# The load of the spread offsets three steps later in a band's chain, with its reader left in place

## The chip, the cores and the metric

The kernel runs on one core of a Trainium2 chip. The metric is the device time of one execution in microseconds. The core's engines are TensorE (PE, with its weight loads shown as PEld), VectorE (DVE), ScalarE (ACT), GpSimd (POOL) and SyncE (SP), which here only issues DMAs.

## The reference

Two layers run one after the other on a batch of 32 images of 96 channels and 56 x 56 pixels, in float32.

- Layer 0: a 1x1 convolution to 576 channels, batch norm, SiLU; a depthwise 3x3 convolution, batch norm, SiLU; a squeeze-and-excite gate; a 1x1 convolution back to 96 channels, batch norm, and the input is added.
- Layer 1: a channel gate from the magnitude of a Fourier transform and a spatial gate from means and that spectrum; the gated image `y`; a 3x3 convolution that gives 18 offsets per pixel and a gate; a plain 3x3 convolution `y_base`; a deformable convolution; a mix of the two; batch norm over the whole batch; the input added; ReLU.

The deformable part is what the change touches:

```python
off = offset.reshape(b, 9, 2, h, w)
px = xx + off[:, :, 0]
py = yy + off[:, :, 1]
sampled = _grid_sample_taps(y, px, py)          # bilinear
y_def = jnp.einsum('bcthw,oct->bohw', sampled, def_w.reshape(c, c, 9))
z = (1 - gate) * y_base + gate * y_def
```

## The kernel before

**Three streams at once.** In `layers`, image `b` is in layer 1's convolutions, image `b+1` in the end of layer 0 and in the gates (`attend`), and image `b+2` in the start of layer 0 (`hidden`). The convolutions are worked off in bands of 8 rows: 7 bands per image, 224 in all. Each band has two halves, each half 7 tiles of 4 columns. For each half TensorE samples the tiles with small matmuls (`sample_tiles`, L738, with transposed blocks from `block_channels`, L724) and then applies the deformable weights (`deform`, L757) into one PSUM tile `pd`, of which there is a single buffer. `combine` (first instruction L796) reads `pd` on VectorE and makes the band's `z`.

**Steps.** After each tile the loop advances two things by one step: `more`, which is the generator `offsets` of the band two ahead (`find(n + 2)`), and `pump()`, which advances the two other streams in proportion to the slots that have passed and runs actions that were put off (`later`). A band advances `more` once at its beginning and 14 times in its halves, so every `yield` in `offsets` is one place between two tiles.

**The chain of one band's offsets.** `offsets` makes the joint convolution on TensorE (L615), copies the 18 offsets to `at` (L664, VectorE), writes them to `od` in DRAM (L668, queue of POOL), makes the rest of `y_base` (L644), takes the largest offset (L675), lets some steps pass, and loads `od` into `ht` (L680, queue of SP). The load spreads each row of `od` to 8 groups of partitions, 252 KB into 112 partitions. After more empty steps it puts off `hats`, which runs two slots later: ScalarE makes `ho` from `ht` (L686, L688) and stores it to `hd` in DRAM (L690, queue of ACT). `ho`'s first instruction is kept in program order on ScalarE.

**The weights.** `prepare` loads, per half band, two `wc` (L702) and one `wr` (L703) from `hd` through the queue of SP; `weights` multiplies them on VectorE (L709, kept in program order), and L738 reads the product. For one half `prepare` needs the `hd` of the next band.

**What else SP issues.** The queue of SP has a fixed order, that of the program text as it is run (`manual_schedule`). Between the loads named above stand those of the other streams: `hq<-h2d` for the 1x1 convolution back (`project_loads`, L311, 784 KB for the first half of the rows and 980 KB for the second, each into a single buffer), `hq<-x1d` for the Fourier transform (L369, 98 KB each, two to a group), `yp<-x1d` and `yp<-fqd` (L594, L606) and `xt` (L213). L329 and L335 are the matmuls that read the first kind, L396 those that read the second. The order on the other engines is made by a scheduler from the program text and priorities.

**Buffers.** `ht` and `ho` have one buffer each; `wc` has three and `wr` two.

Of the kernel before, what the change touches and what calls it, by code (L numbers as in the profile page):

```python
# [628 lines left out]
def joint_conv(nc, p, yp, j, hid):  # L629


    w = p["w"]
    pa = bank(p)
    conv3(nc, pa[:, :BW], w["joint"], yp, CJ, j)
    nc.scalar.activation(hid, pa[:DMID, :BW], AF.Relu, bias=w["dg1b"][:DMID])  # L635
    yb = p["yb"].tile([C, BW], FP, name="yb")
    nc.scalar.activation(yb[BC:], pa[OFF0 + QC :, :BW], AF.Identity, bias=w["cv"]("base_b")[BC:])
    yield yb, pa[OFF0 : OFF0 + NOFF, :BW]
    pb = bank(p)
    for k in range(NTAP):  # L640
        dy, dx = divmod(k, 3)
        r0 = j * RB + dy + PD - 1
        for i in range(2):
            nc.tensor.matmul(pb[i * BC : (i + 1) * BC, : BW // 2].rearrange("p (h w) -> p h w", h=RB // 2), w["base"][:, k],  # L644
                             yp[:C, r0 + i * RB // 2 : r0 + (i + 1) * RB // 2, dx + PD - 1 : dx + PD - 1 + W],
                             start=(k == 0), stop=(k == NTAP - 1))
    yield
    for i in range(2):
        nc.scalar.activation(yb[:BC, i * BW // 2 : (i + 1) * BW // 2], pb[i * BC : (i + 1) * BC, : BW // 2], AF.Identity,  # L649
                             bias=w["cv"]("base_b")[:BC])  # L650
    yield


def offsets(nc, p, yp, j, top, hid, ybs, hds, defer):

    w = p["w"]
    joint = joint_conv(nc, p, yp, j, hid)
    yb, pa = next(joint)  # L660
    ybs.append(yb)
    at = p["off"].tile([NOFF, NTX, 2, TP], FP, name="at")
    for s in range(2):
        nc.vector.tensor_copy(at[:, :, s].rearrange("o t (r c) -> o t r c", r=TS),  # L664
                              pa[:, s * BW // 2 : (s + 1) * BW // 2].rearrange("o (r t c) -> o t r c", r=TS, t=NTX))
    yield
    od = p["dp"].tile([NTX, 2, NOFF, TP], FP, name="od")
    nc.gpsimd.dma_start(od.rearrange("t s o p -> o (t s) p"), at.rearrange("o t s p -> o (t s) p"))  # L668
    yield
    next(joint)  # L670
    yield
    next(joint)
    yield
    next(joint, None)
    nc.vector.tensor_reduce(top, at.rearrange("o t s p -> o (t s p)"), AX.X, ALU.max, apply_absolute_value=True)  # L675
    for _ in range(4):
        yield
    ht = p["ht"].tile([SB * NTX, 4, KP], FP, name="ht")
    src = od.rearrange("t s o p -> t (s o p)").unsqueeze(0).to_broadcast([SB, NTX, 4 * KP])
    nc.sync.dma_start(ht.rearrange("q n k -> q (n k)"), src)  # L680
    for _ in range(6):
        yield

    def hats():
        ho = p["ht"].tile([SB * NTX, 2, 2, KP], FP, name="ho")
        p["tc"].keep_in_program_order(nc.scalar.activation(  # L686
            ho.rearrange("q x s n -> q s x n"), ht.rearrange("q (s x) n -> q s x n", s=2), AF.Abs, bias=w["blk"]))
        nc.scalar.activation(ho, ho, AF.Relu, bias=w["one"], scale=-1.0)  # L688
        hd = p["dp"].tile([2, 2, SB, NTX, KP], FP, name="hd")
        nc.scalar.dma_start(hd.rearrange("x s i t n -> (i t) (x s) n"), ho.rearrange("q x s n -> q (x s) n"))  # L690
        hds.append(hd)

    defer(hats)
# [259 lines left out]
def layers(tc, a, dp, x1d, zd, stats, far):  # L953
# [8 lines left out]
    with ExitStack() as ctx:  # L962
# [127 lines left out]
        def find(n):  # L1090
            if n % 2 == 0:
                hids.append(p["hid"].tile([2 * NS, BW], FP, name="hid"))
            hid = hids[n // 2][n % 2 * NS : n % 2 * NS + DMID]
            return offsets(nc, p, yp, bands[n][1], top[:, n % NBD : n % NBD + 1], hid, ybs, hds,
                           lambda hats: later.append((slot + 2, hats)))
# [420 lines left out]
```

## Time and profile before

| | |
|---|---|
| median of 3 runs | 9001.68 us (8979.61 to 9002.55) |
| profiled execution, own time | 8993.57 us |
| its span | 8991.8 us |
| mean granted TensorE clock | 0.94 |
| PE busy | 8180.0 us (91% of the span) |
| DVE busy | 7174.8 us (80%) |
| ACT busy | 5380.8 us (60%) |
| POOL busy | 2600.4 us (29%) |
| queue of SP (q1) | 985.20 MB, 46.7% of 16 DMA engines' span |
| queue of ACT (q10) | 329.80 MB, 10.2% |
| queue of POOL (q0) | 162.60 MB, 6.7% |

Busy times are of one execution and overlap between engines. In the lists of waits each line names the engine and line that stood idle, what ended the idle time, and then the total in us, the number of times and the longest. In the timeline the columns are start, duration, engine, line, operation, output and inputs, with the idle time before it and what ended it in brackets. In the table by windows each engine's busy time and count of instructions is followed by the granted clock, the share of the DMA engines and GB/s.

### The profile page before, as it was taken

The numbers are of one execution on the slowest core, as the hardware profiler recorded it, in microseconds if no ns is written. First come the engines' busy times: TensorE is split into PE (matmuls) and PEld (weight loads), VectorE is DVE, ScalarE is ACT, GpSimd is POOL, SyncE is SP. The second block draws the span as 40 slices with busy tenths as digits, with TensorE's granted clock in tenths as the row PEclk, the third lists the DMA queues.
The fourth block names the chain that finished last, engine by engine and source line by source line (L and its number), as shares of the span: only waits on it lengthen the run. The fifth ranks groups of instructions, "written<-read, shape, count | busy, mean of one in ns | idle before, by whom it ended". The sixth has DMA issues, their size and how long they took to land. (4 is left out here: it accounts for less than half of the span.)

```text
span 8991.8 us, 137403 instructions
## 1 busy us (share of the span) xinstructions
PE 8180.0 (91%) x52406; PEld 5185.1 (58%) x52406; DVE 7174.8 (80%) x6821; ACT 5380.8 (60%) x10486; POOL 2600.4 (29%) x2608
## 2 busy tenths in 40 slices
PE   5899999999999999999999999999999999999960
PEld 3456565666656656665666666566566656666640
DVE  7688888888888888888888888888888888887333
ACT  2356666666666666666666666666666666666553
POOL 0133233333323332332332333233333323332210
PEclk9889999999999999999999999999999999999985
DMA  2356666666666666666666666666666666666669
GB/s 80 109 144 167 164 167 164 164 155 155 169 167 167 169 163 150 159 164 167 169 167 160 153 159 166 168 167 168 164 151 162 166 166 168 168 165 146 130 189 417
DMA packets 1068756, 1486.47 MB, mean 165 GB/s; under 512 B 590190, under 2 KB 839838, under 8 KB 1055806
## 3 DMA queue, kind: packets, MB, share of 16 engines
q1 hardware_dynamic: 858995, 985.20, 46.7%
q10 hardware_dynamic: 153803, 329.80, 10.2%
q0 software_dynamic: 55296, 162.60, 6.7%
q8 instruction: 420, 6.88, 0.4%
q14 instruction: 242, 1.98, 0.1%
HBM read 1064.29 MB, written 412.65 MB: 164 GB/s over the span
## 5 line engine op out<-in xcount | busy, mean ns | idle before, releaser
L262 DVE SCALAR_TENSOR_TENSOR acch<-hp,w,acch 128x1512 f32<-128x1512 f32 (+1 forms) x2250 | 4348.3, 1933 | 38.3
L615 PE MATMUL mm<-yp,c_jointW 104*128 104x448 f32 x4032 | 1655.9, 562 | 1.0 <-DMA yp<-fqd 1.0
L720 POOL COPY ybl<-yp 96x448 f32<-96x448 f32 x896 | 1035.1, 1183 | 1541.2 <-PE mm L724 1541.0
L757 PE MATMUL pd<-v,c_def 128*96 128x224 f32 (+1 forms) x6272 | 1429.6, 375 | 53.8 <-DVE z L796 29.0
L757 PEld LDWEIGHTS pd<-v,c_def 128*96 128x96 f32 (+1 forms) x6272 | 1039.5, 173 | 349.1 <-issue 74.5
L615 PEld LDWEIGHTS mm<-yp,c_jointW 104*128 104x128 f32 x4032 | 768.0, 194 | 758.2 <-issue 724.7
L738 PE MATMUL mm<-wc,yt 64*96 64x144 f32 x12544 | 1086.6, 302 | 115.7 <-ACT yb L649 44.8
L738 PEld LDWEIGHTS mm<-wc,yt 64*96 64x96 f32 x12544 | 845.6, 165 | 430.2 <-issue 193.2
L173 ACT ACTIVATE hp<-mm,sh,inv 128x392 f32<-128x392 f32 (+2 forms) x1216 | 812.0, 672 | 461.9 <-PE mm L169 416.4
L169 PE MATMUL mm<-xt,w 96*128 96x392 f32 (+3 forms) x2688 | 1056.8, 527 | 34.4 <-DMA xt<-in_x 33.4
L742 ACT COPY v<-mm 96x288 f32<-96x288 f32 (+1 forms) x2688 | 1003.6, 442 | 126.9 <-PE mm L738 81.4
L329 PE MATMUL mm<-hq,w3s 128*96 128x392 f32 x2048 | 796.8, 536 | 99.2 <-DMA hq<-h2d 92.4
L709 DVE TENSOR_TENSOR wc<-wc,wr 128x1008 f32<-128x1008 f32 x448 | 562.7, 1256 | 365.8 <-DMA wr<-hd 338.6
L644 PE MATMUL mm<-yp,c_base0W 96*64 96x224 f32 x8064 | 827.3, 357 | 0.0
L668 POOL DMA_DIRECT2D od<-at x224 | 185.6, 829 | 2217.9 <-DVE at L664 1515.6
L749 ACT COPY v<-v 32x448 f32<-32x448 f32 x1344 | 755.2, 562 | 29.7
L644 PEld LDWEIGHTS mm<-yp,c_base0W 96*64 96x64 f32 x8064 | 554.0, 135 | 275.4 <-issue 61.5
L726 ACT COPY yt<-mm 128x384 f32<-128x384 f32 (+1 forms) x896 | 350.5, 439 | 544.3 <-PE mm L724 543.8
L635 ACT ACTIVATE hid<-mm,c_dg1b 50x448 f32<-50x448 f32 x224 | 140.6, 628 | 862.9 <-PE mm L615 853.6
L329 PEld LDWEIGHTS mm<-hq,w3s 128*96 128x96 f32 x2048 | 339.1, 174 | 453.1 <-issue 311.0
L222 ACT ACTIVATE acch<-acch,sh,inv 128x1568 f32<-128x1568 f32 x288 | 488.3, 1695 | 180.3 <-DVE acch L262 167.0
L476 POOL TENSOR_TENSOR o<-o,xc 96x392 f32<-96x392 f32 x256 | 374.3, 1462 | 738.9 <-ACT o L339 737.3
(194 smaller groups left out, 9146.8 us busy)
## 6 DMA issues: line engine op xcount, KB each, us to landing
h2d<-acch ACTq DMA_DIRECT2D x288, 784.0 KB
wc<-hd SPq DMA_DIRECT2D x896, 252.0 KB
wr<-hd SPq DMA_DIRECT2D x448, 504.0 KB
hq<-h2d SPq DMA_DIRECT2D x128, 980.0 KB
hq<-h2d SPq DMA_DIRECT2D x128, 784.0 KB
hq<-x1d SPq DMA_DIRECT2D x768, 98.0 KB
ht<-od SPq DMA_DIRECT2D x224, 252.0 KB
hd<-ho ACTq DMA_DIRECT2D x224, 252.0 KB
```

The costliest lines, as they stand in the source:

```text
L169: nc.tensor.matmul(pt[p0 : p0 + w1.shape[1], : rows * W], w1, xts[hf][:, r0 * W : (r0 + rows) * W], start=True, stop=True)
L173: nc.scalar.activation(h1[lo:hi, row0 : row0 + rows, 1 : 1 + W], pt[lo:hi, : rows * W].rearrange("p (h w) -> p h w", h=rows), AF.Silu, bia ...
L262: nc.vector.scalar_tensor_tensor(acc[:, lo:hi], win, wk, acc[:, lo:hi], ALU.mult, ALU.add)
L329: nc.tensor.matmul(pts[half][:C, :EW], w3s[:, ch], hq, start=(i == 0), stop=False)
L615: nc.tensor.matmul(view, weights[:, k], yp[:channels, r0 : r0 + RB, dx + PD - 1 : dx + PD - 1 + W], start=(k == 0), stop=(k == NTAP - 1))
L644: nc.tensor.matmul(pb[i * BC : (i + 1) * BC, : BW // 2].rearrange("p (h w) -> p h w", h=RB // 2), w["base"][:, k], yp[:C, r0 + i * RB // 2 ...
L709: p["tc"].keep_in_program_order(nc.vector.tensor_tensor(wc, wc, wr, ALU.mult))
L720: nc.gpsimd.tensor_copy(yb[:, :, s], blocks)
L738: nc.tensor.matmul(pt[k][:C, (t - lo) * KP : (t - lo + 1) * KP], yt[ps, t], s[ps, t * KP : (t + 1) * KP], start=True, stop=True)
L742: nc.scalar.copy(v[:C, :, lo:hi, k].rearrange("c k t p -> c t k p"), pt[k][:C, : (hi - lo) * KP].rearrange("c (t k p) -> c t k p", t=hi - ...
L749: nc.scalar.copy(v[C:, 1 + 2 * i : 3 + 2 * i], v[i * QC : (i + 1) * QC, KA:])
L757: nc.tensor.matmul(out.rearrange("c q (t x) -> c t q x", x=TS), p["w"]["def"][ks, k], v[ks, k].rearrange("c t s (r x) -> c t (s r) x", r=T ...
```

## The change

In `offsets` the load of `ht` is issued after seven empty steps and followed by three, where it was issued after four and followed by six. The number of steps in the chain is the same, and `hats`, which reads `ht`, runs in the same slot as before. Nothing else in the program text differs.

```diff
     nc.vector.tensor_reduce(top, at.rearrange("o t s p -> o (t s p)"), AX.X, ALU.max, apply_absolute_value=True)
-    for _ in range(4):
+    for _ in range(7):
         yield
     ht = p["ht"].tile([SB * NTX, 4, KP], FP, name="ht")
     src = od.rearrange("t s o p -> t (s o p)").unsqueeze(0).to_broadcast([SB, NTX, 4 * KP])
     nc.sync.dma_start(ht.rearrange("q n k -> q (n k)"), src)
-    for _ in range(6):
+    for _ in range(3):
         yield
```

## The prediction

> **What bounds the kernel now.** First the page: which engine is full, and at what clock.
>
> ```profile
> PE 8180.0 (91%) x52406; PEld 5185.1 (58%) x52406; DVE 7174.8 (80%) x6821; ACT 5380.8 (60%) x10486; POOL 2600.4 (29%) x2608
> PE   5899999999999999999999999999999999999960
> PEclk9889999999999999999999999999999999999985
> ```
>
> TensorE is busy 9 tenths or more in slices 3 to 38, the fused stage in which the change lies. So a microsecond counts there only if PE gets or loses it. Second, the waits between engines, for who stops PE and who waits for the load that moves, and third the waits of the SP queue:
>
> ```profile
> PE mm L329 <- DMA hq<-h2d: 92.4, 30, 4.1
> ACT ho L686 <- DMA ht<-od: 98.6, 32, 4.2
> DVE wc L709 <- DMA wr<-hd: 338.6, 120, 15.7
> PE pd L757 <- DVE z L796: 29.0, 25, 3.0
> ```
>
> ```profile
> SPq L680 <- DMA od<-at: 1573.5, 160, 21.9
> SPq L311 <- PE mm L329: 698.0, 96, 13.4
> ```
>
> PE's largest wait of all is for an hq load, about 3.1 us once per image; ACT waits as often, and as long, for ht. SP itself waits 1573.5 us at L680, but SP computes nothing: that wait matters only for what is queued behind it. Fourth, the timeline of one image around the place where these waits meet:
>
> ```profile
> 4139.47 0.37 SPq L311 DMA_DIRECT2D hq<-h2d  x1
> 4139.89 1.22 SPq L702 DMA_DIRECT2D wc<-hd  x2
> 4141.21 0.54 SPq L703 DMA_DIRECT2D wr<-hd  x1
> 4141.85 0.66 SPq L680 DMA_DIRECT2D ht<-od  x1
> 4144.75 9.08 SPq L311 DMA_DIRECT2D hq<-h2d  x2
> ...
> 4156.02 0.78 ACT L686 ACTIVATE ho<-ht,c_blk 112x576 f32<-112x576 f32 x1 [3.68 <-DMA ht<-od]
> ...
> 4157.64 0.35 ACTq L690 DMA_DIRECT2D hd<-ho  x1
> 4157.98 4.29 PE L329 MATMUL mm<-hq,w3s 128*96 128x392 f32 x8 [3.72 <-DMA hq<-h2d]
> ...
> 4169.92 1.19 SPq L702 DMA_DIRECT2D wc<-hd  x2
> ...
> 4180.73 1.21 DVE L709 TENSOR_TENSOR wc<-wc,wr 128x1008 f32<-128x1008 f32 x1 [3.85 <-DMA wr<-hd]
> ...
> 4187.85 0.68 DVE L796 SCALAR_TENSOR_TENSOR z<-pd,c_cvec,yb 96x448 f32<-96x448 f32 x1
> ...
> 4188.59 0.62 PE L757 MATMUL pd<-v,c_def 96*96 96x224 f32 x2 [1.95 <-DVE z L796]
> ```
>
> Read it as a chain: ht lands, ACT makes ho, stores hd, SP loads wc and wr from it, DVE multiplies them (L709), three L262 later forms z (L796), and z frees the one pd bank that PE's L757 needs. I read the same place in the 29 images of full overlap: ho starts 13.95 us after ht's issue, L329 15.9, L709 37.8, z 45.4, L757 46.2, each within about 1.5 us. PE waits 3.1 us at L329 and again 1.3 us at L757. So the stretch ends when the chain from ht ends, not when the hq load lands.
>
> **The change, part by part.** The chain keeps its 10 empty steps (4+6 becomes 7+3), and the order of instructions on PE is the same, instruction by instruction, in both programs. On SP the ht load is ordered differently in only 62 of 224 bands; in the other 162 no SP instruction lies in those three steps, and I cost them at nothing. ACT and POOL differ in one place each near the end; DVE swaps a few reductions and one L602 after z in 15 images, neighbours of 0.7 to 1.8 us, costed at 0 with 2 us per image (30 us) in the upper end.
>
> (a) 30 times (once per image, the place shown), ht is issued behind the next 784 KB hq load. That load waits for PE's L329 to free its buffer (4144.75), so ht is issued at about 4145.2 instead of 4141.85. Both transfers wait for the wc and wr loads before them, so what is exchanged is their order in the queue, not 3.3 us. In the old order ACT could start on ht at 4156.02 and PE on hq at 4157.98, 1.96 us apart; the mean over the images is 1.97. The same bytes in front of the later one: ht should end where hq did, **1.9 us later**; hq ends earlier by 1.9 us to 3 us (ht's packets occupy the trace for 3 us). PE is ready at 4154.26, so L329's wait falls from 3.1 to between 0 and 1.2 us; I take 0.6, a gain of 2.5.
>
> The wait has a second price, the clock. Windows after this place and after an L757:
>
> ```profile
> 4157.50:4160.90 3.40, 2.92 (x5) 1.47 (x6) 3.33 (x3) 1.85 (x4) 2.35 (x2) 0.50 1.13 282
> 4447.60:4454.40 6.80, 6.80 (x23) 5.20 (x24) 6.18 (x9) 2.73 (x6) 1.57 (x3) 0.50 1.06 226
> ```
>
> The granted clock is 0.50 for 3.4 or 6.8 us after every one of the 29 L329 waits, and after 12 of the 29 L757 waits, those of 1.4 to 3.1 us. A spell of 3.4 to 6.8 us at half speed, less some 0.7 us still idle, loses about 2.2 us at L329. So PE reaches L757 earlier by 2.5+2.2 = **4.7 us**.
>
> It finds nothing there. L757 goes when z is made, and that chain began with ht. Of ho's 1.9 us delay, the part that reaches wr is unknown. Upper bound 1.9: everything shifts. Lower bound 0: the hd store took 11.9 us from issue to landing while the wc and wr loads issued before it at 4156.13 and 4157.46 still drained; if it lands with them in any case, nothing shifts. Below 0 there is no reason, as ho only gets later. I take 0.5, nearer to the drained end, because hd's last part landed within 0.7 us of that wr: 30 x 0.5 = 15 us.
>
> L757's wait becomes 1.3+4.7+0.5 = 6.5 us, twice the L329 wait that was always followed by half clock. What that costs the end can be read off: where the clock dropped after L757 the first joint convolution some 120 us later came 122.4 us after L757 (12 images), otherwise 119.7 (17), so 2.7 us. After the change 30 spells of about 2.5 us against 12 of 2.7: 75-32 = 43 us. The Trainium skill ("TensorE: Matmul & The Clock Gate", Part 1) says the clock halves only after a whole idle window of about 3.4 us. The rows speak against that threshold: waits of 1.4 us were enough here. By the rule alone the old L757 waits would be free and 30 new ones not, 75 us in place of 43; I keep the rows.
>
> (b) 30 times ht is issued behind six hq<-x1d loads (98 KB each). In the image shown ht went at 4180.96 and the first of these at 4183.67, because x1d was not yet written; in all 30 they start 1.1 to 6.4 us after ht. They were not held up by ht, so they gain nothing. ht gets later: the sixth has landed 14.4 us after ht's old issue, ht some 2 us behind it, at 16.4; ACT takes ho at 19.5 in its order and idles 0.03 us before it. Hidden with 3 us to spare; without that cover 30 x 2 = 60 us. SP's wait for od (about 9 us each here) goes and turns into the wait for x1d.
>
> Who else is behind ho on ACT: two L339, the hd store and two L173. PE next needs them at the L738 of 4169.72, some 10 us after they would be done. No cost.
>
> Sum: the profiled execution took 8993.57 us (span 8991.8 and 1.8 around it). 15 + 43 + 0 = +58, so 9052. The median of the runs, 9001.68, lies 8 us above the profiled execution; on that footing, **9060**.
>
> **Rivals.** *The gain arrives (faster).* If z at L796 does not hold PE, the 4.7 us per image stay: 30 x 4.7 = 141, about 8860. For it: L329 is PE's biggest wait in the list. Against it: PE waits at L757 now, before any gain, and DVE reaches L709 early and idles 2.4 us for wr. It decides only if wr lands over 4 us earlier than now; a part of that gives a part of the gain. 0.17.
>
> *A trade without a balance.* hd lands with the drained queue, and the half-clock spells after L757 replace those after L329 at no extra loss: 0, 9002. Against it are the 2.7 us. 0.23.
>
> *The other place fails too (slower still).* If ht in (b) lands after 19.5 us, ACT, which works in order, stops, and through it PE: 3 us each, 90 us on top, about 9150. It decides once the six loads take 5 us longer than they did. 0.10.
>
> **How the numbers follow.** The forecast has 0.50. Its own range: 0 to 57 us for the chain and 0 to 70 us for the clock (30 x 3.4 less 32), so 9002 to 9129. To hold 8 in 10 the range takes in the trade and a small gain below, 8975, and part of the second failure above, 9135. A measurement here tells about 0.3% (27 us) from no change: slower 0.50+0.10 = 0.60, within 0.23, faster 0.17.
>
> **What would show it.** Right: PE's wait at L329 for hq falls from 92.4 to under 35 us in total; ACT's wait for ht grows from 98.6 to about 155; the waits at L757 grow to 5 us or more per image with half clock behind each; L796 comes 0 to 2 us later after the hq issue than now. Wrong: the L757 wait stays near 1.3 us while L329's is gone (the gain arrived), wr lands 3 us later or more, ACT waits for ht in (b), or PE waits at a place that is not named here.

## The result, and the profile after

The changed kernel is slower: 9029.27 us, median of 7 runs (9018.67 to 9043.28), against 8987.61 us for the kernel before (7 runs, 8973.15 to 9009.64). The ratio is 1.0045, with a 95% interval of 1.0032 to 1.0059. The profiled executions took 9038.34 us (span 9036.6, clock 0.936) after and 8993.57 us (8991.8, 0.940) before.

First the page of the changed kernel, its busy times:

```profile
PE 8204.2 (91%) x52406; PEld 5205.8 (58%) x52406; DVE 7191.0 (80%) x6821; ACT 5383.2 (60%) x10486; POOL 2618.6 (29%) x2608
```

PE has the same 52406 instructions and is busy 24 us longer: the same work at a lower clock. Next its waits between engines:

```profile
PE mm L329 <- DMA hq<-h2d: 62.1, 31, 4.2
ACT ho L686 <- DMA ht<-od: 173.1, 34, 7.7
DVE wc L709 <- DMA wr<-hd: 347.3, 119, 15.4
PE pd L757 <- DVE z L796: 94.4, 28, 6.5
```

L329 gained 30 us (92.4 before), L757 lost 65 us (29.0), ACT waits 74 us longer for ht (98.6), and DVE's wait for wr is as it was (338.6). The waits of the SP queue show the moved load from the other side:

```profile
SPq L680 <- DMA od<-at: 1256.4, 125, 21.9
SPq L369 <- DMA x1d<-o: 383.9, 46, 16.9
```

SP waits 317 us less for od (1573.5 before) and 255 us more for x1d (129.4 before): at place (b) the one wait is exchanged for the other. Now the timeline of the same image as in the prediction, at place (a):

```profile
4156.31 0.54 SPq L703 DMA_DIRECT2D wr<-hd  x1
4159.85 0.36 SPq L311 DMA_DIRECT2D hq<-h2d  x1
4160.32 0.67 SPq L680 DMA_DIRECT2D ht<-od  x1
...
4171.47 4.41 PE L329 MATMUL mm<-hq,w3s 128*96 128x392 f32 x8 [2.11 <-DMA hq<-h2d]
...
4173.06 0.78 ACT L686 ACTIVATE ho<-ht,c_blk 112x576 f32<-112x576 f32 x1 [5.62 <-DMA ht<-od]
4174.68 0.33 ACTq L690 DMA_DIRECT2D hd<-ho  x1
...
4184.49 1.20 SPq L702 DMA_DIRECT2D wc<-hd  x2
...
4195.30 1.21 DVE L709 TENSOR_TENSOR wc<-wc,wr 128x1008 f32<-128x1008 f32 x1 [3.27 <-DMA wr<-hd]
...
4202.54 0.68 DVE L796 SCALAR_TENSOR_TENSOR z<-pd,c_cvec,yb 96x448 f32<-96x448 f32 x1
...
4203.28 1.06 PE L757 MATMUL pd<-v,c_def 96*96 96x224 f32 x2 [2.91 <-DVE z L796]
```

Count from the wr issue of each trace (4141.21 before, 4156.31 here). L329 starts at 15.2 instead of 16.8 and hd is stored at 18.4 instead of 16.4; yet the next wc load is issued at 28.2 instead of 28.7, z comes at 46.2 instead of 46.6 and L757 at 47.0 instead of 47.4. The middle of the chain has moved, its end has not, and L757 waits 2.91 us where it waited 1.95. The table by windows, right behind this L757:

```profile
4203.30:4206.70 3.40, 3.40 (x12) 2.71 (x13) 3.30 (x7) 1.58 (x4) 0.52 (x1) 0.50 0.95 215
```

A clock of 0.50 over 3.4 us follows the wait. The means over 30 images, in us after that wr issue (the anchor), for both kernels and for six of the experiments below; those of half clock, spells and period are over 29 images. "Half clock" is the PE time lost to it (PE's busy time at clock 0.50, halved) between the anchor and L757 and in the 14 us behind L757; a spell is a half-clock stretch that begins between 4 us before L757 and 7 us after it (of the 25 in the changed kernel, 15 begin before L757).

| | hd stored | hd landed | wr landed | z | L757 | wait at L757 | half clock ahead of / behind L757 | spells in 29 | image period |
|---|---|---|---|---|---|---|---|---|---|
| before | 16.16 | 28.06 | 38.51 | 45.81 | 46.65 | 1.26 | 2.15 / 1.17 | 12 | 262.01 |
| after | 18.67 | 28.06 | 38.50 | 45.82 | 46.60 | 3.42 | 1.12 / 2.57 | 25 | 263.59 |
| after, L757's wait filled | 18.66 | 28.02 | 38.46 | 45.92 | 47.02 | 0.78 | 1.11 / 0.40 | 7 | 261.36 |
| before, L329's wait filled | 16.11 | 28.07 | 38.30 | 45.40 | 46.21 | 2.28 | 0.00 / 2.02 | 23 | 262.48 |
| earlier ht | 12.28 | 18.91 | 32.77 | 42.43 | 43.55 | 0.22 | 1.65 / 0.18 | 3 | 262.51 |
| earlier ht, sums on DVE | 12.28 | 19.02 | 32.82 | 42.15 | 43.53 | 0.09 | 1.76 / 0.00 | 0 | 258.14 |
| sums on DVE only | 16.16 | 27.94 | 38.45 | 44.10 | 45.50 | 0.12 | 2.28 / 0.06 | 1 | 260.54 |
| only place (a) | 18.69 | 27.89 | 38.25 | 45.66 | 46.44 | 3.27 | 1.09 / 2.44 | 24 | 263.31 |

The image period grew by 1.58 us; over the 29 images that is 46 us, and the two profiled executions differ by 44.8. All of it lies behind L757: from L757 to the next anchor 215.19 us before, 216.79 after. Of these 1.60 us, 1.40 are the growth of the half clock in the 14 us behind L757 (1.17 to 2.57).

### The profile page after: what moved, and what is told of

Read it like the earlier page. It is cut to its first block, busy times and chain, and to the rows that moved or that the text cites. A ratio compares the mean times of both kernels' runs of the same rounds, so it can differ in the third digit from the quotient of the medians.

```text
span 9036.6 us, 137448 instructions
## 1 busy us (share of the span) xinstructions
PE 8204.2 (91%) x52406; PEld 5205.8 (58%) x52406; DVE 7191.0 (80%) x6821; ACT 5383.2 (60%) x10486; POOL 2618.6 (29%) x2608
## 3 DMA queue, kind: packets, MB, share of 16 engines
q14 instruction: 243, 1.99, 0.1%
## 5 line engine op out<-in xcount | busy, mean ns | idle before, releaser
L262 DVE SCALAR_TENSOR_TENSOR acch<-hp,w,acch 128x1512 f32<-128x1512 f32 (+1 forms) x2250 | 4359.3, 1937 | 38.4
L757 PE MATMUL pd<-v,c_def 128*96 128x224 f32 (+1 forms) x6272 | 1464.8, 382 | 118.5 <-DVE z L796 94.4
L757 PEld LDWEIGHTS pd<-v,c_def 128*96 128x96 f32 (+1 forms) x6272 | 1059.7, 176 | 425.0 <-issue 103.1
L738 PE MATMUL mm<-wc,yt 64*96 64x144 f32 x12544 | 1088.8, 302 | 103.4 <-ACT hp L173 42.1
L738 PEld LDWEIGHTS mm<-wc,yt 64*96 64x96 f32 x12544 | 847.9, 165 | 417.9 <-issue 199.1
L709 DVE TENSOR_TENSOR wc<-wc,wr 128x1008 f32<-128x1008 f32 x448 | 562.4, 1255 | 374.0 <-DMA wr<-hd 347.3
L329 PE MATMUL mm<-hq,w3s 128*96 128x392 f32 x2048 | 767.0, 519 | 63.5 <-DMA hq<-h2d 62.1
L476 POOL TENSOR_TENSOR o<-o,xc 96x392 f32<-96x392 f32 x256 | 376.9, 1472 | 794.3 <-ACT o L339 792.3
L329 PEld LDWEIGHTS mm<-hq,w3s 128*96 128x96 f32 x2048 | 328.7, 169 | 403.0 <-issue 375.5
```

The costliest lines, as they stand in the source:

```text
L262: nc.vector.scalar_tensor_tensor(acc[:, lo:hi], win, wk, acc[:, lo:hi], ALU.mult, ALU.add)
L329: nc.tensor.matmul(pts[half][:C, :EW], w3s[:, ch], hq, start=(i == 0), stop=False)
L709: p["tc"].keep_in_program_order(nc.vector.tensor_tensor(wc, wc, wr, ALU.mult))
L738: nc.tensor.matmul(pt[k][:C, (t - lo) * KP : (t - lo + 1) * KP], yt[ps, t], s[ps, t * KP : (t + 1) * KP], start=True, stop=True)
L757: nc.tensor.matmul(out.rearrange("c q (t x) -> c t q x", x=TS), p["w"]["def"][ks, k], v[ks, k].rearrange("c t s (r x) -> c t (s r) x", r=T ...
```

## Experiments

My theory: the chain from hd over wr to z fixes L757, PE's time gained at L329 is waited off there, and the longer wait costs clock behind it. The rivals are named in each expectation. Ratios are to the kernel before, run on the same chip, with 95% intervals.

**The two places apart.** The step count becomes an argument `pre` of `offsets`, chosen by band, with `n % 7 == 1` for place (a) in one kernel (the lines below are against the changed kernel) and `n % 7 == 2` for place (b) in the other:

```diff
-    for _ in range(7):
+    for _ in range(pre):
         yield
...
-    for _ in range(3):
+    for _ in range(10 - pre):
         yield
...
-                           lambda hats: later.append((slot + 2, hats)))
+                           lambda hats: later.append((slot + 2, hats)), 7 if n % 7 == 1 else 4)
```

> The later load only in the bands of place (a) (n % 7 == 1, 7 steps before it and 3 after), 4 and 6 in all others. Theory (the prediction's steps with the terms as the two traces show them): the whole loss comes from here, about 1.5 us per image behind L757, so 40 to 46 us and a ratio of 1.0040 to 1.0055 to the kernel before; ACT's wait for ht about 170 us, PE's wait at L757 about 95 us, as in the changed kernel. Rival (the loss comes from place (b), or from the reductions that DVE takes in another order): 1.000 to 1.002.

> The later load only in the bands of place (b) (n % 7 == 2), 4 and 6 in all others. Theory: ht lands 2 to 3 us before ACT comes to it, nothing moves, ratio 0.9985 to 1.0010, ACT's wait for ht stays near 99 us and PE's wait at L757 near 54 us over all its releasers. Rival: the loss comes from here, 1.003 to 1.006, with ACT's wait for ht grown by 1 us or more in these 30 bands.

Place (a) alone gave 1.0038 (1.0025 to 1.0051), place (b) alone 1.0008 (0.9996 to 1.0019). The waits of the kernel with (a) alone are those of the changed kernel:

```profile
ACT ho L686 <- DMA ht<-od: 173.2, 32, 6.8
PE pd L757 <- DVE z L796: 84.3, 26, 5.8
```

and those of the kernel with (b) alone are those of before, within 20 us:

```profile
ACT ho L686 <- DMA ht<-od: 90.8, 32, 4.4
PE pd L757 <- DVE z L796: 46.3, 27, 4.6
```

So place (a) carries the loss: 1.0038 of 1.0045. For (b) the interval leaves anything from nothing to 17 us. In the trace of (b) alone L757 at place (a) waited 1.70 us with 17 spells, against 1.26 us and 12 before, although place (a) is unchanged there; whether that is chance or an effect of (b), one profiled execution does not tell. At (b) ht lands 9 us ahead of ACT's turn for it (50.3 against 59.7 us in the changed kernel), further ahead than the 3 us I had counted.

**Is the loss clock?** Eight matmuls that nobody reads, just ahead of the L757 of each image's first band, keep PE at work through the wait:

```diff
+def warm(nc, p, v, k):
+    pw = bank(p) if k else None
+    for _ in range(k): nc.tensor.matmul(pw[:C, : BW // 2], p["w"]["def"][:C, 0], v[:C, 0], start=True, stop=True)
...
             if h == 0:
+                warm(nc, p, v, 8 if n % NBD == 0 else 0)
                 pds[n] = p["pd"].tile([128, 512], FP, name="pd")
```

> The changed kernel with eight extra matmuls (96x96 by 224 columns, about 0.36 us each, 2.9 us in all) into an unused PSUM bank, just ahead of L757 in the first half of the first band of each image, so that PE works during the 3.5 us wait that the change left there. The result of these matmuls is read by nobody. DVE takes some reductions in another order. Theory (the loss is half clock after the wait): PE's idle time at L757 falls to below 1 us per image, the half-clock spells behind it from 25 of 29 to 12 or fewer, and 30 to 45 us of the loss come back: ratio to the kernel before 0.999 to 1.002. Rival (the loss is something else that begins with the later ht): the ratio stays at 1.0045 or grows.

The ratio is 0.9989 (0.9973 to 1.0005): the whole loss is gone, with ht, hd, wr and z where the changed kernel has them (table, third row). Its waits and the group of the extra matmuls (L763; L757 follows z, which stands at L798 here):

```profile
PE pd L757 <- DVE z L798: 23.5, 16, 2.8
```
```profile
L763 PE MATMUL mm<-v,c_def 96*96 96x224 f32 x512 | 102.3, 353 | 0.2 <-ACT v L742 0.2
```

PE does 102.3 us more work and the kernel is 47 us faster than the changed one, the half clock behind L757 having fallen from 2.57 to 0.40 us per image.

**The same loss without moving a transfer.** If PE's time at L329 is worth nothing there, it should also be worth nothing when it is gained in another way. In the kernel before, six unused matmuls fill the wait at L329:

```diff
         mine = [(ch, hq) for ch, hq in rows[half] if ch < NCH - 1]
+        for _ in range(6 if last and half == 0 else 0): nc.tensor.matmul(pts[half][:C, :EW], w3s[:, 0], p["w"]["def"].rearrange("c k o -> c (k o)")[:, :EW], start=True, stop=True)
...
-            outs = project(nc, p, rows)
+            outs = project(nc, p, rows, q + 1 == NQ)
```

> The kernel before with ht in its old place, and six extra matmuls (128 deep, 96 by 392 columns, about 0.5 us each, 3.1 us in all) ahead of the L329 that waits for its hq load, into the bank that L329 then starts afresh; nobody reads them. No transfer moves. They fill the 3.2 us wait, and with it goes the half clock behind it (2.15 us of PE time before L757). Theory (the chain ht, hd, wr, z holds L757, and PE time gained at L329 is worth nothing or less): L757 keeps its place at 46.7 us after the anchor, its wait grows from 1.3 to 2.5 us or more, and the spells behind it cost as in the changed kernel: ratio 1.001 to 1.005 although the clock is better at L329. Rival (PE's own time sets the end, and the changed kernel lost for another reason): L757 comes 1.5 to 2 us earlier, 45 to 60 us, 0.993 to 0.996.

The ratio is 1.0020 (1.0005 to 1.0036). PE loses no clock at all ahead of L757, and the kernel is slower for it: L757 starts at 46.21 in place of 46.65, waits 2.28 us, and 23 of 29 images have the spell. Waits of this kernel:

```profile
PE mm L329 <- DMA hq<-h2d: 2.1, 1, 2.1
PE pd L757 <- DVE z L796: 60.0, 26, 4.3
```

92 us of wait became 2, 29 became 60, and the time went up. This is the changed kernel's exchange without a moved transfer.

**Does the chain move if ht is early enough?** The opposite shift, 2 steps before the load and 8 behind it in place (a), puts ht ahead of that half's wc and wr:

> The opposite shift: in the bands of place (a) the load of ht after 2 steps and 8 behind it, so that SP issues it ahead of the wc and wr loads of that half, the others 4 and 6. ACT's wait for ht there (3.1 us per image) goes in both theories. Theory 1, the prediction's chain (the end of the stretch is set by ht): hd is stored up to 3.1 us earlier, wr and z follow, the 1.3 us wait at L757 and its 1.2 us of half clock go: 30 x 2.5 = 75 us faster, ratio 0.990 to 0.994. Theory 2 (hd lands when the queued loads have drained, whenever it was issued, as its landing 28.05 us after the anchor in the changed kernel against 28.08 suggests): wr and L757 keep their time, ratio 0.998 to 1.002.

Ratio 1.0001 (0.9988 to 1.0013). By the time theory 2 seemed right, by the trace it was not: hd, stored 3.9 us earlier, landed 9.2 us earlier, wr 5.7 us and L757 3.1 us earlier (table; the wr issue from which these are counted is itself some 0.8 us later here, since ht goes ahead of it). Stored at 12.3, ahead of the wc and wr loads of 15.0, hd needed 6.6 us; stored at 16.2 or 18.7, behind them, it landed at 28.06 in either case. The time came out even because of another wait, which the waits of this kernel show:

```profile
DVE sq L379 <- DMA hq<-x1d: 131.3, 38, 6.0
PE mm L738 <- DVE sq L379: 64.9, 31, 2.3
PE mm L396 <- DVE sq L379: 17.4, 21, 1.5
PE pd L757 <- DVE z L796: 6.0, 6, 1.4
```

L757's wait is gone, and PE waits 82 us for L379, which waits for the Fourier loads of x1d. Those wait for the store of the last sums `o` (L476, POOL). The timeline of this kernel around such a sum, and then the same sum in the kernel before:

```profile
4169.58 1.83 DVE L262 SCALAR_TENSOR_TENSOR acch<-hp,w,acch 128x1568 f32<-128x1568 f32 x1
4169.61 5.70 POOL L476 TENSOR_TENSOR o<-o,xc 96x392 f32<-96x392 f32 x1 [0.48 <-ACT o L339]
...
4171.55 1.13 DVE L709 TENSOR_TENSOR wc<-wc,wr 128x1008 f32<-128x1008 f32 x1
4172.61 6.88 DVE L262 SCALAR_TENSOR_TENSOR acch<-hp,w,acch 128x1568 f32<-128x1568 f32 x3
```
```profile
4174.84 1.83 DVE L262 SCALAR_TENSOR_TENSOR acch<-hp,w,acch 128x1568 f32<-128x1568 f32 x1
...
4175.18 2.37 POOL L476 TENSOR_TENSOR o<-o,xc 96x392 f32<-96x392 f32 x1 [0.80 <-ACT o L339]
```

The mean of this sum is 5.1 us with the earlier ht and 2.1 us before. In the kernel before DVE works beside the first 1.7 us of this sum and then falls idle for wr (3.85 us, up to the L709 of 4180.73), and the sum ends 0.7 us later; over the images DVE is busy for 68% of the sum's time. With wr early, DVE works on (99%), and the sum takes more than twice as long. The start of the x1d loads went from 42.7 to 43.7 us.

**Taking that sum away from POOL.** First one of the two last sums of each image on DVE, then both:

```diff
-                nc.gpsimd.tensor_tensor(o, o, xr, ALU.add)
+                (nc.vector if q == NQ - 1 and k < NQ else nc.gpsimd).tensor_tensor(o, o, xr, ALU.add)
```

> The earlier ht in the bands of place (a) (2 steps before, 8 behind), and of the last two sums o of each image (L476) the first on DVE in place of POOL; DVE takes it ahead of the first of the two L709. In the kernel with the earlier ht alone this sum took 5.1 us on POOL, DVE then waited 4.1 us for the Fourier load of x1d at L379 and PE 2.1 us for L379, with 1.2 us of half clock behind it. Theory (that sum gives the gain back): L379's wait falls under 1.5 us, PE's wait for L379 from 82 us in total under 25, and 30 x 2 to 3 us arrive: ratio 0.990 to 0.995. Rival (the load of x1d is late for its queue, or PE stops at the delayed L709 instead): 0.998 to 1.003.

A miss: 1.0001 (0.9987 to 1.0015). The second sum, still on POOL beside the same DVE work, now took 5.5 us, and the x1d loads started at 43.65 as before. With `k >= 0`, that is both sums on DVE:

> The earlier ht in the bands of place (a), and both of the last two sums o of each image (L476) on DVE in place of POOL; DVE takes them ahead of the first of the two L709. With only the first of them on DVE the second, on POOL, took 5.5 us, and the Fourier loads came no earlier. Theory (those sums on POOL, slow beside a busy DVE, give the gain of the earlier ht back): the loads of x1d start 2 us earlier than with the earlier ht alone (41.7 in place of 43.7 us after the anchor), L379's wait falls from 4.1 under 2 us, PE's wait for L379 from 82 us in total under 30, ratio 0.991 to 0.996. Rival (the 1.3 us more on DVE cost as much, or PE stops at the delayed L709): 0.998 to 1.003.

The ratio is 0.9868 (0.9854 to 0.9883), 8864.3 us: faster than both kernels, and more than I expected. The x1d loads start at 40.1 us, and of the two waits a rest is left: 36.5 us in total for L379 (131.3 with the earlier ht alone) and 11.8 us for PE's L738 behind it (64.9).

How much of this is the place of ht? The sums on DVE alone, with ht in its old place:

> The kernel before with ht in its old place, and only the last two sums o of each image (L476) on DVE in place of POOL. On DVE one L262 of 1.8 us comes ahead of the two L709 with them, so that two L262, not three, stand between the second L709 and z. Theory (ht's chain still ends with wr at 38.5 us after the anchor, so L709 cannot start before): z is made near 44 us in place of 45.8, L757's wait of 1.3 us shrinks under 0.5, some 1.5 to 2.5 us per image arrive, ratio 0.991 to 0.996, and 40 to 60 us are missing to the kernel that has the earlier ht as well (0.9868). Rival (the sums and the order on DVE made the whole gain, the place of ht nothing): 0.9855 to 0.9885, as with both.

0.9915 (0.9898 to 0.9932). The chain keeps its time up to wr (38.45), z comes 1.7 us earlier by the order on DVE, as expected, and L757's wait all but goes. The earlier ht is worth the rest, 42 us by the two ratios (0.9915 and 0.9868, whose intervals do not meet). The two medians, 8936.24 and 8864.3, differ by 72 us, but they come from two chips, on which the kernel before has 9002.51 and 8986.13. Without the sums on DVE the earlier ht was worth nothing.

**Filled waits with the earlier ht.** Five unused matmuls ahead of the waiting L329, then five more ahead of L757:

> The earlier ht in the bands of place (a), and five extra matmuls (128 deep, 96 by 392 columns, about 0.5 us each, 2.6 us in all) ahead of the L329 that waits for its hq load, into the bank that L329 then starts afresh; nobody reads them. They fill the 2.5 us wait. Theory (the image is held by a chain that begins with PE's L329 and L335 of that load: o, its store, the loads of x1d, L379): the half clock after L329 (1.65 us of PE time between the anchor and L757) falls under 0.6, all that follows comes 1 us earlier: 20 to 45 us, ratio 0.995 to 0.998. Rival (the end is set by DMA queues or by DVE, and PE's clock here is hidden): 0.999 to 1.002.

> The earlier ht in the bands of place (a), five extra matmuls ahead of L329 (2.6 us, as in the kernel with the earlier ht and the filled L329) and five (96 deep, 96 by 224, about 0.36 us each, 1.8 us in all) ahead of the L757 of the first band of each image. Nobody reads any of them. The first five alone left a wait of 2.0 us at L757 with 1.66 us of half clock behind it. Theory (what is left there is clock, and a filled wait keeps it): the half clock behind L757 falls under 0.6 us, 30 x 1 us arrive on top: ratio 0.994 to 0.997. Rival: 0.998 or more.

0.9981 (0.9967 to 0.9995) and 0.9967 (0.9955 to 0.9978): the first just outside its theory's range, the second inside. The first moved a wait as in the kernel before: L757 came 0.9 us later, not earlier, and waited 1.99 us, with 21 spells. The second took the spells away (none in 29), but the two intervals overlap, so its own gain is not clear of the noise. In both, the last sum on POOL took 2.8 us where it took 5.1 with the earlier ht alone, so how much of the gain is clock and how much is that sum stays open.

**A cut that was not one.** To take the chain away altogether, the weights of place (a) were loaded from the hd of the band before, with the old and with the new place of ht:

```diff
-                loads.append(weights_load(nc, p, hds[n], m))
+                loads.append(weights_load(nc, p, hds[n - (n % 7 == 1 and m == 0)], m))
```

> The kernel before, with the chain cut behind hd in the bands of place (a): the wc and wr of the first half of these bands are loaded from the hd of the band before (so the sampling weights there are those of the wrong band; all sizes and instructions are the same), and SP does not wait for the new hd. Theory: wr lands 10 us or more earlier, L757's wait of 1.3 us goes, but as in the kernel with the earlier load DVE then runs on while POOL makes the last sum o (L476), that sum takes 4 to 6 us in place of 2.1, the Fourier loads of x1d come later and PE waits some 2 us for L379: ratio 0.997 to 1.002. Rival (L757 alone held the image): 30 x 2.5 = 75 us faster, 0.990 to 0.993.

> The changed kernel with the same cut (weights of the wrong band in the first half of the bands of place (a)). Against the cut kernel before it differs only in the later ht. Theory: with no chain behind ht, PE's shorter wait at L329 (2.0 us in place of 3.2) and 1.0 us less of half clock behind it are kept, since o, its store and the loads of x1d follow from L335: 30 x 1 to 2.2 us, 30 to 66 us faster than the cut kernel before, the ratio to the uncut kernel before 0.990 to 0.998. Rival (the time saved at L329 is lost at some other wait whatever becomes of the chain, or the later ht costs by itself): no faster than the cut kernel before.

0.9984 (0.9967 to 1.0001) and 1.0010 (0.9998 to 1.0023). The second fell on the side of its rival: the cut kernel with the later ht is not faster. But the cut did not hold. The SP queue of the cut kernel before:

```profile
4148.94 13.31 SPq L702 DMA_DIRECT2D wc<-hd  x2
```

The first wc load goes at 4148.94, the second only at 4161.67, when hd has landed; in the trace it carries the same completion semaphore as hd's store. So wr still came after hd (landed at 35.9 and 37.4 us after the anchor, 38.5 without the cut), and with the later ht L757 still waited 2.80 us. These two runs don't tell whether a gain at L329 arrives when nothing holds L757.

## Why the prediction was right, point by point

The forecast was slower, 9060 us in a range of 8975 to 9135; 9029 came. Its mechanism was right: PE's gain at L329 is waited off at L757, and the longer wait costs clock. Two of its terms were off. Of the four signs named for it, L796 kept its place (45.81 and 45.82 us), as forecast, and ACT's wait for ht grew, to 173.1 us where about 155 was forecast; L329's wait fell to 62.1 us in total, not under 35, and L757's grew to 3.4 us per image, not 5, with half clock behind 25 of 29. None of the signs of being wrong came.

- **The places.** (a) costs (1.0038 alone); for (b) no cost is shown (1.0008, an interval that holds 1). The reading that ht did not hold up the Fourier loads at (b) was off: in the kernel with (b) alone they started at 41.2 us, not 42.7, without a gain in time. Why, no run shows.
- **ht and hq change order.** ht landed 2.5 us later (1.9 forecast), hq only 1.2 us earlier (1.9 to 3), so L329's wait fell from 3.2 to 2.0 us, not to 0.6. With the half clock ahead of L757 (2.15 to 1.12) PE gained 2.2 us, not 4.7. The step that failed is "the same bytes in front": in the trace an ht load posts 8 completions as its data lands (after one post about 1 us behind its issue) and an hq load 16, and in the image shown, before the change 8 of hq's 16 had already come (4152.52 to 4154.77) when the first of ht's 8 came (4154.88). Half of hq seems not to have been behind ht at all. The Trainium skill ("DMA: Bandwidth & Descriptors", section "Why a DMA increments its semaphore by 16 and not by 1") says a transfer uses the largest number of engines, up to 16, that divides the outer sizes of both its sides, which would make these 8 and 16. No run here changed the shape of either load, so this reading is argued and not shown.
- **The chain.** I took 0.5 us of ho's delay for wr, between 0 and 1.9: a term of 15 us. It was 0: hd landed at 28.06 in both kernels. The drained queue was the right reason, but the weight I gave to the other bound was not; hd moved only when its store was issued ahead of the wc and wr loads, as the earlier ht showed.
- **L757's wait** was forecast at 6.5 us and came to 3.4, since only 2.2 us were gained, not 4.7.
- **The clock.** Forecast 43 us, from 2.7 us per half-clock event. From L757 to the next anchor 1.60 us were lost per image, 48 us over 30. That the size came out right was in part luck: there were 25 spells, not 30, but each cost 3.0 us of PE time in the 14 us behind L757, not 2.5. Filling the wait brought the whole loss back, so that the loss is clock is shown.
- **The threshold.** The Trainium skill ("TensorE: Matmul & The Clock Gate", Part 1) lets the clock fall after an idle window of about 3.4 us. The runs speak against that as a threshold. Over the 14 kernels and 29 images of each, a spell came with none of the 205 waits at L757 under 1 us, with 2 of 18 from 1 to 1.4 us, with 50 of 71 from 1.4 to 2 us, and with 108 of 112 from 2 us on. The change comes near 1.4 to 2 us, and nothing changes at 3.4.
- **The rivals.** *The gain arrives* fell with the unmoved L757 and with the filled L329 of the kernel before. *A trade without a balance* was near in its first half (the chain term is 0) and wrong in its second. *The other place fails too* fell with (b) alone.
- **The median.** 14 of the 31 us by which the forecast was high come from the base: 9001.68 us in 3 runs became 8987.61 in 7.

## What to carry to other kernels

A wait that is the longest in the list is not the one to shorten if a second chain ends just behind it: look at the next place where the same engine waits, and ask what that place waits for. A wait that is only moved can still change its price, since clock is lost behind it; unused matmuls that fill a fixed wait are a cheap way to tell idle time from clock. When a chain is shortened and the time stays, look for what had been working in the idle time that went: here the end of POOL's sum had fallen into DVE's wait.

## What the runs showed of the hardware that was not expected

- A store's landing time depended more on the loads issued before it than on its own issue: hd issued 2.5 us later, behind the same wc and wr loads, landed at the same 28.06 us, and issued 3.9 us earlier, ahead of them, 9.2 us earlier.
- The same sum on POOL (96x392) took 2.1 us on the mean with DVE busy for 68% of it and 5.1 us with DVE busy for 99%, on L262 and L709 for the most part, instructions with two tensor inputs. The Trainium skill ("SBUF — State Buffer", section "Who interferes with whom") says such a DVE instruction and a GpSimd instruction that reads SBUF hold each other off. The rows agree in direction, and taking the sums off POOL made the kernel with the earlier ht 1.3% faster. A busy DVE alone does not set the size: with L329's wait filled and the earlier ht, the sum took 2.8 us beside a DVE that was busy all the time.
- PE can be given more work and the kernel gets faster: 102.3 us of unused matmuls took 47 us off the changed kernel.
